# Where the side work of an attention unit stands on TensorE: two blocks, and three operands in the scores' rotation

## The chip, the core and the metric

The kernel runs on one core of a Trainium2 chip. The metric is device time in microseconds (us). Three runs of the kernel before gave 3573.38 us as their median (3570.64 to 3573.6). The engines are called PE (TensorE's matmuls), PEld (its weight loads), DVE (VectorE), ACT (ScalarE), POOL (GpSimd) and SP (SyncE, which issues DMAs here). They run side by side and wait for each other through semaphores.

## The reference

Two layers on x of shape (8, 2048, 256), with one matrix adj of 2048 x 2048. Layer 0 is a graph convolution with two linear maps and batch norms, and a layer norm of x plus its result. Layer 1 is masked attention with four heads, again with a residual and a layer norm:

```python
def _L1_gnn_ref(h, W, adj):
    ...
    qkv = h @ W
    qkv = qkv.reshape(Bn, Nn, 3, H, HEAD_DIM).transpose(2, 0, 3, 1, 4)
    q, k, v = (qkv[0], qkv[1], qkv[2])
    mask = jnp.where(adj == 0, -jnp.inf, 0.0)
    scores = jnp.einsum('bhid,bhjd->bhij', q, k) / np.sqrt(HEAD_DIM) + mask
    attn = jax.nn.softmax(scores, axis=-1)
    out = jnp.einsum('bhij,bhjd->bhid', attn, v)
    return out.transpose(0, 2, 1, 3).reshape(Bn, Nn, OUT_DIM)

# --- layer 0 (adj_resnorm) ---
x = _layernorm(x + _L0_gnn_ref(x, adj, ...), axis=-1)
# --- layer 1 (adj_resnorm) ---
x = _layernorm(x + _L1_gnn_ref(x, L1_gnn_W, adj), axis=-1)
```

All values are float32. The change touches layer 1 alone, and in it the end of layer 0's norm (its second linear map's result, called y, is normalised, added to x and layer-normalised inside the attention loop).

## The kernel before

The attention is cut into 64 *units*: 8 batches x 2 pairs of heads (hp) x 4 chunks (c) of 512 query rows. A unit has 16 *steps*, one for each 128 rows of keys, so there are 1024 steps g in all. In a step PE multiplies K and Q into a tile of scores (`scores`, L910: four matmuls in four 64 x 64 quarters of the array, eight records each step), DVE adds the mask (`mask_scores`, L922), ACT takes the exponential (L928), and three steps later (LEAD = 3) PE weighs V with it (`weigh`, L940, four quarters again). POOL adds up the probabilities for the softmax's sums (L950 to L961), with DMAs that add one tile into another.

PSUM, where PE writes, is full: the scores' tiles are `st` from the pool ps_s with two buffers of two banks each; the weighed sum is `out_ps` from ps_o with one buffer of two banks; everything else is `pm` from ps_m with two buffers of one bank each. A tile of a pool takes the place of the one before the last of its name, and waits until that one's readers have ended. Waits are kept by tile.

Beside that each unit has *side work*, in calls listed by `at_step(u, j, f, ...)`: the call is made in unit u at step int(j); calls of one step are sorted by j. If j is whole the call stands between the scores and their mask, otherwise behind the exponential. All engines but SP keep the order in which the program is written.

The side work on PE, all with the full height of the array, is:

- `finish_sums` (L977): the sums of the unit before, four matmuls with a 128 x 32 block of ones; ACT copies the result to sm (L985).
- `finish_turn_sums` (L991): two transposes of sm; DVE copies the sums and takes their reciprocal (L993, L998).
- `finish_turn` (L1004) and `finish` (L1012): four transposes of the unit's result ot, and eight small multiply-adds on DVE in two halves.
- `project` (L845 for Q and K, L859 for V): Q, K and V of a later chunk from the turned input x1t. ACT empties Q (L850) and V (L866), DVE empties K (L854).
- `norm` (L779): y of the next batch is transposed in two halves of four transposes into a pm tile, and DVE adds x (L787) and takes the layer norm's statistics (L728, L730). `turn` (L808) transposes the normalised x; ACT copies it to x1t (L814).

In a steady unit these stood in up to four places: Q at step 0 (with the second half of y), sums, K and y's first half at step 6, the turning of sums, V and the turning of ot at step 10, and the turning of x at step 13. Where a unit ends, `finish_out` copies and adds the two halves of out_ps to ot on ACT and DVE (L965, L966) before the next unit's first weighing may overwrite them. The loop that sets the order is:

```python
if j == NT - 1:
    weigh(g)
    finish_out(u)
tasks = side.get((u, j), ())
for i, f, args in tasks:
    if i == j:
        f(*args)
if ahead:
    mask_scores(g + LEAD, st)
    exps(g + LEAD)
for i, f, args in tasks:
    if i > j:
        f(*args)
if j < NT - 1:
    weigh(g)
```

Of the kernel before, what the change touches and what calls it, by code (L numbers as in the profile page):

```python
# [8 lines left out]
F32 = mybir.dt.float32  # L9
# [17 lines left out]
def tile_gcn_then_masked_attention(  # L27
# [15 lines left out]
    nc = tc.nc  # L43
    ENG = mybir.EngineType
    PSUM = bass.MemoryType.PSUM
    P = 128
    B, N, D = x.shape
# [7 lines left out]
    CH = 512  # L55
    NCH = N // CH
    TPC = CH // P
    NALL = B * NCH
    HP = D // P
# [138 lines left out]
    with tc.tile_pool(name="bt7", bufs=1, side="right") as bp7, tc.tile_pool(  # L198
        name="stage", bufs=2, side="right"
    ) as sp, tc.tile_pool(name="stage1", bufs=1, side="right") as sp1, tc.tile_pool(  # L200
        name="pst", bufs=4, space=PSUM
# [17 lines left out]
        for n, t in enumerate(order):  # L219
# [9 lines left out]
            here = slice(q * P, (q + 1) * P)  # L229
# [52 lines left out]
    with tc.tile_pool(  # L282
        name="psa", bufs=4, space=PSUM
# [147 lines left out]
        for v, (k, b, d) in enumerate(units):  # L431
            first, last = v == 0, v == len(units) - 1
            turn = not last and units[v + 1][0] != k
            w = v + 1
# [114 lines left out]
        for name, size in (  # L549
            ("h1", [P, NH, CH]), ("dbc", [P, 2, CH]), ("w1f", [P, 4, H // 2])  # L550
        ):
            t = lp.tile(size, F32, name=name).rearrange("p a b -> p (a b)")
# [156 lines left out]
    IT = BR // P  # L709
    NU = B * HP * NCH  # L710
# [5 lines left out]
    class LayerNorm:  # L716
# [9 lines left out]
        def stats(self, tiles):  # L726
            for i in tiles:
                nc.vector.bn_stats(self.st[:, i, :], self.t[:, i, :])  # L728
            for i in tiles:
                nc.vector.bn_aggr(self.mv[:, i, :], self.st[:, i, :])  # L730
# [14 lines left out]
    class Layer1Input:  # L745
# [23 lines left out]
        def norm(self, b, c, half):  # L769
            pm = self.psum.tile([P, IT, D], F32, name="pm")  # L770
            self.turn_y(b, c, half, pm)
            self.add_y(b, c, half, pm, self.x1[b, c])

        def turn_y(self, b, c, half, pm):
            y = self.yt[b, c]
            for i in range(IT):
                r0 = (IT * half + i) * P
                for o in range(NO):
                    nc.tensor.transpose(  # L779
                        pm[:, i, o * P : (o + 1) * P], y[:, o, r0 : r0 + P], ident  # L780
                    )
# [31 lines left out]
            r0 = c * CH + half * BR  # L813
            nc.scalar.copy(self.x1t[b][:, :, r0 : r0 + BR], pm)  # L814

        def emit_stats(self, b, c, half):
            if half == 0:
                self.ln[b, c] = LayerNorm(self.pool, self.x1[b, c])
            self.ln[b, c].stats(range(IT * half, IT * (half + 1)))
# [8 lines left out]
            if half:  # L828
                nc.sync.dma_start(rows(b, c, out), self.x1.pop((b, c)))

        def project(self, b, hp, c, which, k_on_act=False):

            if (b, hp) not in self.qkv:
                self.qkv[b, hp] = (
                    self.pool.tile([P, N], F32, name="qt"),
                    self.pool.tile([P, N], F32, name="kt"),
                    self.pool.tile([P, NT, P], F32, name="v"),
                )
            xt = self.x1t[b]
            cols = slice(c * CH, (c + 1) * CH)  # L840
            wcols = slice(which * D + hp * P, which * D + (hp + 1) * P)
            pm = self.psum.tile([P, CH], F32, name="pm")
            if which < 2:
                for d in range(ND):
                    nc.tensor.matmul(  # L845
                        pm, wq[:, d, wcols], xt[:, d, cols], start=(d == 0), stop=(d == ND - 1)
                    )
                dst = self.qkv[b, hp][which][:, cols]
                if which == 0:
                    nc.scalar.activation(dst, pm, AF.Copy, scale=HD**-0.5)  # L850
                elif k_on_act:
                    nc.scalar.copy(dst, pm)
                else:
                    nc.vector.tensor_copy(dst, pm)  # L854
            else:
                for j in range(TPC):
                    t = c * TPC + j
                    for d in range(ND):
                        nc.tensor.matmul(  # L859
                            pm[:, j * P : (j + 1) * P],  # L860
                            xt[:, d, t * P : (t + 1) * P],
                            wq[:, d, wcols],
                            start=(d == 0),
                            stop=(d == ND - 1),
                        )
                nc.scalar.copy(  # L866
                    self.qkv[b, hp][2][:, c * TPC : (c + 1) * TPC, :].rearrange(
                        "p t d -> p (t d)"
                    ),
                    pm,  # L870
                )
# [5 lines left out]
    def attention():  # L877


        with tc.tile_pool(  # L880
            name="attn_in", bufs=2, side="left", reuse_waits="tile"
        ) as ip, ExitStack() as late, tc.tile_pool(
            name="ps_s", bufs=2, space=PSUM, reuse_waits="tile"
        ) as ps_s, tc.tile_pool(
            name="ps_o", bufs=1, space=PSUM, reuse_waits="tile"
        ) as ps_o, tc.tile_pool(
            name="ps_m", bufs=2, space=PSUM, reuse_waits="tile"
        ) as ps_m:
            inp = Layer1Input(ip, ps_m, NCH + 4)
# [148 lines left out]
            def at_step(u, j, f, *args):  # L1038
                tasks = side.setdefault((u, int(j)), [])
                tasks.append((j, f, args))  # L1040
                tasks.sort(key=lambda task: task[0])

            per_b = HP * NCH
            for u in range(NU):
                b, hp, c = units[u]
                at_step(u + 1, 6, finish_sums, u)
                at_step(u + 1, 10, finish_turn_sums, u)
                at_step(u + 1, 10.2, finish_turn, u)
                at_step(u + 1, 10.3, finish, u, 0)
                at_step(u + 1, 11.1, finish, u, 1)  # L1050
                if u == NU - 2:
                    for half in range(2):
                        at_step(u + 1, 11.3 + half, inp.emit_stats, b, c, half)
                        at_step(u + 1, 14 + half, inp.emit, b, c, half)
                    at_step(u + 1, 12.5, inp.root, b, c)
                elif u == NU - 1:
                    for half in range(2):
                        at_step(u + 1, 10.4 + half, inp.emit_stats, b, c, half)
                        at_step(u + 1, 10.5 + half, inp.root_half, b, c, half)
                        at_step(u + 1, 12 + half, inp.emit_half, b, c, half)  # L1060
                    at_step(u + 1, 14, count_sums)
                elif hp == HP - 1:
                    for half in range(2):
                        at_step(u + 1, 12.5 + 1.5 * half, inp.emit_stats, b, c, half)
                        at_step(u + 2, 4 + half, inp.emit, b, c, half)
                    at_step(u + 1, 15.5, inp.root, b, c)

            PROJECT = (0.2, 6.1, 10.1)  # L1070

            def project_at(u, b, hp, c):
                for w in range(3):
                    at_step(u, PROJECT[w], inp.project, b, hp, c, w)

            for b in range(B):
                u0 = b * per_b
                if b:
                    project_at(u0, b, 0, NCH - 1)
                for c in range(NCH):  # L1080
                    project_at(u0 + 1 + c, b, 1, c)
                    if b + 1 == B:
                        continue
                    u = u0 + 3 + c
                    at_step(u, 1, inp.load_y, b + 1, c)
                    at_step(u, 1, inp.load_x, b + 1, c)
                    for o in range(NO):
                        at_step(u, 3.5 + 1.2 * o, inp.bn, b + 1, c, o)
                    at_step(u, 6.2, inp.norm, b + 1, c, 0)
                    at_step(u + 1, 0.1, inp.norm, b + 1, c, 1)  # L1090
                    at_step(u + 1, 3, inp.root, b + 1, c)
                    for half in range(2):
                        at_step(u + 1, 7 + half, inp.apply, b + 1, c, half)
                        at_step(u + 1, 13 + 0.2 * half, inp.turn, b + 1, c, half)
                    if c < NCH - 1:
                        project_at(u + 2, b + 1, 0, c)

# [8 lines left out]
            ):  # L1106
                at_step(0, j, inp.project, 0, 0, c, w)
            for c in (2, 3):
                at_step(c - 1, 3.1, inp.project, 0, 0, c, 0)

            with tc.manual_schedule(engines=IN_ORDER):
                for c in range(NCH):
# [37 lines left out]
                for g in range(NU * NT):  # L1150
                    u, j = divmod(g, NT)
                    ahead = g + LEAD < NU * NT
                    if ahead:
                        st = scores(g + LEAD)
# [22 lines left out]
    def attention_with_maxima():  # L1177

        with tc.tile_pool(name="full", bufs=2) as ap_, tc.tile_pool(
            name="full_s", bufs=2, space=PSUM  # L1180
        ) as ps_s, tc.tile_pool(name="full_o", bufs=2, space=PSUM) as ps_o, tc.tile_pool(
            name="full_m", bufs=2, space=PSUM
# [5 lines left out]
            inp = Layer1Input(ap_, ps_m, NCH)  # L1188
            for b in range(B):
# [12 lines left out]
                for hp in range(HP):  # L1202
# [4 lines left out]
                    for t in range(NT):  # L1207
                        for h in range(2):
# [23 lines left out]
                            for j in range(NT):  # L1232
                                pm = ps_m.tile([P, P], F32, name="pm")
# [10 lines left out]
                            )  # L1244
                for c in range(NCH):
                    for half in range(2):
                        inp.emit_stats(b, c, half)
                    inp.root(b, c)
                    for half in range(2):
                        inp.emit(b, c, half)  # L1250

    attention()


    n_bad = nc.values_load(bad[0:1, 0:1])
    with tc.If(n_bad > 0):
        attention_with_maxima()
# [43 lines left out]
```

## Time and profile before

| What | us |
|---|---|
| Median of the runs | 3573.38 |
| The profiled execution, its own time | 3573.89 |
| Its span, from the first to the last instruction | 3571.8 |
| Busy: PE / DVE / ACT / POOL | 3524.8 / 2112.7 / 1575.7 / 2335.5 |
| L922, the masks on DVE, 1024 of 1.215 | 1239.1 |
| L928, the exponentials on ACT, 1024 of 1.056 | 1081.2 |
| L940 and L910, weighings and scores on PE | 1075.0 and 1063.6 |
| L845, Q and K; L859, V | 253.0; 125.1 |

The profile is one execution, recorded by instruction. The attention's first scores stand at 1251 us and its last weighings at 3542 us, so it holds some 2290 us of the span. Scores, weighings and the side work share PE. A float32 matmul is two records; a transpose is one. The four quarter matmuls of a step overlap, so that eight records of 0.59 us fill about 0.86 us. In timelines, a group's length runs to the modelled end of its last record and overlaps the next group; the distance from start to start is the time a group really takes of PE. Idle time in square brackets is that of the engine before the group, with what ended it.

### The profile page before, as it was taken

The numbers are of one execution on the slowest core, as the hardware profiler recorded it, in microseconds if no ns is written. First come the engines' busy times: TensorE is split into PE (matmuls) and PEld (weight loads), VectorE is DVE, ScalarE is ACT, GpSimd is POOL, SyncE is SP. The second block draws the span as 40 slices with busy tenths as digits, with TensorE's granted clock in tenths as the row PEclk, the third lists the DMA queues.
The fourth block names the chain that finished last, engine by engine and source line by source line (L and its number), as shares of the span: only waits on it lengthen the run. The fifth ranks groups of instructions, "written<-read, shape, count | busy, mean of one in ns | idle before, by whom it ended". The sixth has DMA issues, their size and how long they took to land. (4 is left out here: it accounts for less than half of the span.)

```text
span 3571.8 us, 55309 instructions
## 1 busy us (share of the span) xinstructions
PE 3524.8 (99%) x22447; PEld 1461.9 (41%) x22447; DVE 2112.7 (59%) x3125; ACT 1575.7 (44%) x1952; POOL 2335.5 (65%) x1590
## 2 busy tenths in 40 slices
PE   8999999999999899999999999999999999999997
PEld 5444444444444433433343433343443334343332
DVE  6224342432356656766766776676676676676666
ACT  5000000000045455665665565565566565566555
POOL 4544364435357556777777787777677777777777
PEclk9999999999999899999999999999999999999999
DMA  9122242231256445666575566566556556655555
GB/s 342 53 77 81 90 159 71 71 100 41 77 228 241 152 83 108 129 126 123 111 149 117 115 130 134 110 137 129 114 124 142 110 122 137 120 114 122 113 113 114
DMA packets 197577, 440.16 MB, mean 123 GB/s; under 512 B 14128, under 2 KB 121152, under 8 KB 186944
## 3 DMA queue, kind: packets, MB, share of 16 engines
q0 software_dynamic: 64656, 239.37, 35.3%
q1 hardware_dynamic: 132048, 196.11, 16.0%
q8 instruction: 178, 2.92, 0.3%
q10 hardware_dynamic: 608, 1.06, 0.1%
q14 instruction: 87, 0.71, 0.1%
HBM read 126.62 MB, written 75.51 MB: 57 GB/s over the span
## 5 line engine op out<-in xcount | busy, mean ns | idle before, releaser
L922 DVE SCALAR_TENSOR_TENSOR prob<-mask,st 128x1024 f32<-128x1024 uint8 x1024 | 1239.1, 1215 | 434.5 <-PE st L910 360.6
L928 ACT ACTIVATE prob<-prob 128x1024 f32<-128x1024 f32 x1024 | 1081.2, 1056 | 913.5 <-DVE prob L922 836.3
L940 PE MATMUL out_ps<-prob,v 64*64 64x512 f32 x8192 | 1075.0, 595 | 3.6 <-DVE ot L966 2.6
L910 PE MATMUL st<-qt,kt 64*64 64x512 f32 x8192 | 1063.6, 589 | 0.1
L961 POOL TENSOR_TENSOR acc<-acc,prob 128x1024 f32<-128x1024 f32 x319 | 830.0, 2602 | 5.7 <-DMA prob<-prob 0.7
L341 PE MATMUL pa<-t,x 128*128 128x512 f32 x1792 | 774.5, 594 | 2.7 <-ACT x L317 2.7
L950 POOL DMA_DIRECT2D prob<-prob x447 | 403.8, 929 | 565.3 <-PE out_ps L940 458.0
L910 PEld LDWEIGHTS st<-qt,kt 64*64 64x64 f32 x8192 | 312.6, 133 | 566.7 <-issue 526.9
L341 PEld LDWEIGHTS pa<-t,x 128*128 128x128 f32 x1792 | 342.1, 191 | 431.9 <-issue 427.7
L940 PEld LDWEIGHTS out_ps<-prob,v 64*64 64x64 f32 x8192 | 290.9, 133 | 542.1 <-issue 469.4
L952 POOL TENSOR_TENSOR acc<-acc,prob 128x1024 f32<-128x1024 f32 x126 | 298.1, 2365 | 7.5
L845 PE MATMUL pm<-x1t,wq 128*128 128x512 f32 x512 | 253.0, 617 | 0.7 <-ACT x1t L814 0.7
L470 POOL TENSOR_TENSOR ag<-ag,dbc 128x512 f32<-128x512 f32 x16 | 20.2, 1263 | 314.5 <-DVE ag L469 287.9
L450 ACT COPY ag<-pa 128x512 f32<-128x512 f32 x16 | 9.4, 588 | 448.2 <-PE pa L341 435.1
L399 ACT COPY h<-ph 128x512 f32<-128x512 f32 x28 | 16.4, 585 | 416.7 <-PE ph L390 416.7
L959 POOL TENSOR_TENSOR acc<-prob 128x1024 f32<-128x1024 f32 x64 | 171.1, 2674 | 3.0 <-DMA prob<-prob 3.0
L740 ACT ACTIVATE x<-x,ln_nm,ln_rs 128x256 f32<-128x256 f32 x256 | 137.6, 586 | 8.7 <-POOL ln_nm L736 8.7
L845 PEld LDWEIGHTS pm<-x1t,wq 128*128 128x128 f32 x512 | 87.9, 191 | 119.5 <-issue 112.8
L1012 DVE SCALAR_TENSOR_TENSOR x<-pm,ri,x 128x64 f32<-128x64 f32 x512 | 109.5, 277 | 44.1 <-PE pm L1004 44.1
L859 PE MATMUL pm<-wq,x1t 128*128 128x128 f32 x1024 | 125.1, 276 | 0.0
L859 PEld LDWEIGHTS pm<-wq,x1t 128*128 128x128 f32 x1024 | 119.4, 192 | 2.5 <-ACT x1t L814 1.7
L966 DVE TENSOR_TENSOR ot<-out_ps,ot 128x512 f32<-128x512 f32 x64 | 44.3, 692 | 124.4 <-ACT ot L965 124.4
(156 smaller groups left out, 2855.8 us busy)
## 6 DMA issues: line engine op xcount, KB each, us to landing
prob<-prob POOLq DMA_DIRECT2D x447, 512.0 KB, 4.9
x<-in_x_dram SPq DMA_DIRECT2D x92, 512.0 KB, 6.6
h_d<-h SPq DMA_DIRECT2D x28, 1024.0 KB, 4.2
t<-h_d SPq DMA_DIRECT2D x28, 1024.0 KB, 7.5
a<-in_adj_dram SPq DMA_DIRECT2D x16, 1024.0 KB, 5.0
y_d<-ag SPq DMA_DIRECT2D x32, 512.0 KB, 2.6
out_dram<-x SPq DMA_DIRECT2D x31, 512.0 KB, 6.8
yt<-y_d SPq DMA_DIRECT2D x28, 512.0 KB, 3.2
```

What stands on the lines that cost most here:

```text
L341: nc.tensor.matmul(pa, s.t[:, m, :], t[:, m, :], start=(m == 0), stop=(m == HT - 1))
L740: nc.scalar.activation(self.t[:, i, :], self.t[:, i, :], AF.Identity, bias=self.nm[:, i : i + 1], scale=self.rs[:, i : i + 1],)
L845: nc.tensor.matmul(pm, wq[:, d, wcols], xt[:, d, cols], start=(d == 0), stop=(d == ND - 1))
L859: nc.tensor.matmul(pm[:, j * P : (j + 1) * P], xt[:, d, t * P : (t + 1) * P], wq[:, d, wcols], start=(d == 0), stop=(d == ND - 1),)
L910: nc.tensor.matmul(st[r * HD : (r + 1) * HD, h, :], kt[hs, j * P + r * HD : j * P + (r + 1) * HD], qt[hs, cols], start=True, stop=True,)
L922: nc.vector.scalar_tensor_tensor(p, mask[:, j, cols][:, None, :].to_broadcast([P, 2, CH]), MASKED, st, op0=ALU.mult, op1=ALU.add,)
L928: nc.scalar.activation(probs[g], probs[g], AF.Exp)
L940: nc.tensor.matmul(outs[u][hs, r, :], inp.qkv[b, hp][2][rs, j, hs], probs[g][rs, h, :], start=(j == 0), stop=(j == NT - 1),)
L950: nc.gpsimd.dma_start(probs[g - 1], probs[g], accum_op=ALU.add)
L952: nc.gpsimd.tensor_add(accs[u], accs[u], probs[g])
L959: nc.gpsimd.tensor_add(accs[v], probs[g - 7], probs[g - 5])
L961: nc.gpsimd.tensor_add(accs[v], accs[v], probs[g - 5])
```

## The change

It moves side work and changes three of its PSUM tiles. What moves:

- The sums' turning, V's projection and ot's turning go from step 10 to step 6, behind the sums and K, so that step 6 holds all of them in one run: L977, K, L991, V, L1004. In the lists of units 61 to 64 (the constant BARE = 61), where no projection is left, turning and finishing stay at steps 10 and 11.
- Q's projection goes from step 0 to 15.2, that is behind the unit's last weighing; for the last chunk of a batch's second pair of heads it goes to 6.6 instead.
- y's two halves are transposed together, behind the last weighing (15.1), by the new `turn_and_add`, first both transposes, then both additions. The turning of x goes from step 13 to 15, the layer norm's statistics to steps 0.1 and 1.1 of the next unit, and the scaling from steps 7 and 8 to 9 and 11.
- K and V share one tile of the scores' name `st` (K in its first half, V in its second), and both halves of y take one such tile, in place of pm tiles.
- The statistics of a finished chunk move to 9.1 and 10.6, its root to 12.5, and its output's scaling and DMA from step 4 to steps 1 and 2 of the unit behind.

`emit_stats` is only renamed to `stats`.

```diff
+        def turn_and_add(self, b, c, pm):
+
+            for half in range(2):
+                self.turn_y(b, c, half, pm[:, IT * half : IT * (half + 1)])
+            for half in range(2):
+                here = slice(IT * half, IT * (half + 1))
+                t = self.x1[b, c][:, here]
+                nc.vector.tensor_add(t, pm[:, here], t)
...
-        def project(self, b, hp, c, which, k_on_act=False):
+        def project(self, b, hp, c, which, k_on_act=False, pm=None):
...
-            pm = self.psum.tile([P, CH], F32, name="pm")
+            if pm is None:
+                pm = self.psum.tile([P, CH], F32, name="pm")
...
+            spare = {}
+
+            def key_projection(u, b, hp, c):
+                spare[u] = ps_s.tile([P, 2, CH], F32, name="st")
+                inp.project(b, hp, c, 1, pm=spare[u][:, 0, :])
+
+            def value_projection(u, b, hp, c):
+                inp.project(b, hp, c, 2, pm=spare.pop(u)[:, 1, :])
+
+            def norm(b, c):
+                inp.turn_and_add(b, c, ps_s.tile([P, TPC, D], F32, name="st"))
+
             per_b = HP * NCH
+
+            BARE = NU - NCH + 1
             for u in range(NU):
                 b, hp, c = units[u]
                 at_step(u + 1, 6, finish_sums, u)
-                at_step(u + 1, 10, finish_turn_sums, u)
-                at_step(u + 1, 10.2, finish_turn, u)
-                at_step(u + 1, 10.3, finish, u, 0)
-                at_step(u + 1, 11.1, finish, u, 1)
+                if u + 1 < BARE:
+                    at_step(u + 1, 6.2, finish_turn_sums, u)
+                    at_step(u + 1, 6.4, finish_turn, u)
+                    at_step(u + 1, 6.5, finish, u, 0)
+                    at_step(u + 1, 7.1, finish, u, 1)
+                else:
+                    at_step(u + 1, 10, finish_turn_sums, u)
+                    at_step(u + 1, 10.2, finish_turn, u)
+                    at_step(u + 1, 10.3, finish, u, 0)
+                    at_step(u + 1, 11.1, finish, u, 1)
...
+                elif hp == HP - 1 and u + 1 < BARE:
+                    for half in range(2):
+                        at_step(u + 1, 9.1 + 1.5 * half, inp.stats, b, c, half)
+                        at_step(u + 2, 1.05 + half, inp.emit, b, c, half)
+                    at_step(u + 1, 12.5, inp.root, b, c)
...
-            PROJECT = (0.2, 6.1, 10.1)
...
             def project_at(u, b, hp, c):
-                for w in range(3):
-                    at_step(u, PROJECT[w], inp.project, b, hp, c, w)
+                last = hp == HP - 1 and c == NCH - 1
+                at_step(u, 6.6 if last else 15.2, inp.project, b, hp, c, 0)
+                at_step(u, 6.1, key_projection, u, b, hp, c)
+                at_step(u, 6.3, value_projection, u, b, hp, c)
...
-                    at_step(u, 6.2, inp.norm, b + 1, c, 0)
-                    at_step(u + 1, 0.1, inp.norm, b + 1, c, 1)
+                    at_step(u, 15.1, norm, b + 1, c)
                     at_step(u + 1, 3, inp.root, b + 1, c)
                     for half in range(2):
-                        at_step(u + 1, 7 + half, inp.apply, b + 1, c, half)
-                        at_step(u + 1, 13 + 0.2 * half, inp.turn, b + 1, c, half)
+                        at_step(u + 1, 0.1 + half, inp.stats, b + 1, c, half)
+                        at_step(u + 1, 9 + 2 * half, inp.apply, b + 1, c, half)
+                        at_step(u + 1, 15, inp.turn, b + 1, c, half)
...
-                at_step(c - 1, 3.1, inp.project, 0, 0, c, 0)
+                at_step(c - 2, (15.2, 6.6)[c - 2], inp.project, 0, 0, c, 0)
```

More of the change, by code (lines that the diff above doesn't have):

```diff
@@ L814, in turn, with stats @@
             nc.scalar.copy(self.x1t[b][:, :, r0 : r0 + BR], pm)
-        def emit_stats(self, b, c, half):
+        def stats(self, b, c, half):
             if half == 0:
@@ L1046, in attention @@
                 at_step(u + 1, 6, finish_sums, u)
-                at_step(u + 1, 10, finish_turn_sums, u)
-                at_step(u + 1, 10.2, finish_turn, u)
-                at_step(u + 1, 10.3, finish, u, 0)
-                at_step(u + 1, 11.1, finish, u, 1)
+                if u + 1 < BARE:
[8 more added lines that the diff above has]
+                    at_step(u + 1, 11.1, finish, u, 1)
                 if u == NU - 2:
                     for half in range(2):
-                        at_step(u + 1, 11.3 + half, inp.emit_stats, b, c, half)
+                        at_step(u + 1, 11.3 + half, inp.stats, b, c, half)
                         at_step(u + 1, 14 + half, inp.emit, b, c, half)
@@ L1057, in attention @@
                     for half in range(2):
-                        at_step(u + 1, 10.4 + half, inp.emit_stats, b, c, half)
+                        at_step(u + 1, 10.4 + half, inp.stats, b, c, half)
                         at_step(u + 1, 10.5 + half, inp.root_half, b, c, half)
@@ L1061, in attention @@
                     at_step(u + 1, 14, count_sums)
+                elif hp == HP - 1 and u + 1 < BARE:
[3 more added lines that the diff above has]
+                    at_step(u + 1, 12.5, inp.root, b, c)
                 elif hp == HP - 1:
                     for half in range(2):
-                        at_step(u + 1, 12.5 + 1.5 * half, inp.emit_stats, b, c, half)
+                        at_step(u + 1, 12.5 + 1.5 * half, inp.stats, b, c, half)
                         at_step(u + 2, 4 + half, inp.emit, b, c, half)
                     at_step(u + 1, 15.5, inp.root, b, c)
-            PROJECT = (0.2, 6.1, 10.1)
             def project_at(u, b, hp, c):
-                for w in range(3):
-                    at_step(u, PROJECT[w], inp.project, b, hp, c, w)
+                last = hp == HP - 1 and c == NCH - 1
+                at_step(u, 6.6 if last else 15.2, inp.project, b, hp, c, 0)
+                at_step(u, 6.1, key_projection, u, b, hp, c)
+                at_step(u, 6.3, value_projection, u, b, hp, c)
             for b in range(B):
@@ L1246, in attention_with_maxima @@
                     for half in range(2):
-                        inp.emit_stats(b, c, half)
+                        inp.stats(b, c, half)
                     inp.root(b, c)
```

## The prediction

> **What bounds the kernel now.** I read the totals first, then the stages, then the order of work on PE inside one attention unit, then the waits.
>
> ```profile
> PE 3524.8 (99%) x22447; PEld 1461.9 (41%) x22447; DVE 2112.7 (59%) x3125; ACT 1575.7 (44%) x1952; POOL 2335.5 (65%) x1590
> L940 PE MATMUL out_ps<-prob,v 64*64 64x512 f32 x8192 | 1075.0, 595 | 3.6 <-DVE ot L966 2.6
> ```
>
> PE is busy 99% of the span, and the weighing line sat idle 3.6 us in 8192 records. The table of stages says the same of the attention alone:
>
> ```profile
> 2000.00:2500.00 500.00, 499.26 (x4195) 198.24 (x4197) 345.98 (x523) 302.62 (x368) 375.57 (x269) 1.00 0.62 127
> ```
>
> Columns after the window: its length, then busy PE, PEld, DVE, ACT, POOL. PE has 0.7 us free of 500, at full clock. So the time is PE's own: its work, what it loses between kinds of work, and any wait that is new. The busy number hides the losses, since matmuls overlap; they show in the starts. PE's timeline (start, length, line, shape, records):
>
> ```profile
> 2006.48 1.04 PE L940 MATMUL out_ps<-prob,v 64*64 64x512 f32 x8
> 2007.34 1.04 PE L910 MATMUL st<-qt,kt 64*64 64x512 f32 x8
> 2008.30 0.44 PE L991 MATMUL pm<-ident,sm 128*128 128x128 f32 x2
> 2008.58 1.95 PE L859 MATMUL pm<-wq,x1t 128*128 128x128 f32 x16
> 2010.36 0.60 PE L1004 MATMUL pm<-ident,ot 128*128 128x128 f32 x4
> 2010.89 1.09 PE L940 MATMUL out_ps<-prob,v 64*64 64x512 f32 x8
> 2011.80 1.04 PE L910 MATMUL st<-qt,kt 64*64 64x512 f32 x8
> ...
> 2021.57 1.04 PE L910 MATMUL st<-qt,kt 64*64 64x512 f32 x8
> 2022.54 0.66 PE L779 MATMUL pm<-ident,yt 128*128 128x128 f32 x4
> 2023.03 1.88 PE L845 MATMUL pm<-x1t,wq 128*128 128x512 f32 x4
> 2024.84 1.09 PE L940 MATMUL out_ps<-prob,v 64*64 64x512 f32 x8
> ...
> 2034.34 1.04 PE L910 MATMUL st<-qt,kt 64*64 64x512 f32 x8
> 2035.31 0.64 PE L977 MATMUL pm<-acc,ones 128*32 128x256 f32 x8
> 2035.87 1.99 PE L845 MATMUL pm<-x1t,wq 128*128 128x512 f32 x4
> 2037.69 0.60 PE L779 MATMUL pm<-ident,yt 128*128 128x128 f32 x4
> 2038.22 1.09 PE L940 MATMUL out_ps<-prob,v 64*64 64x512 f32 x8
> ```
>
> Scores and weighings follow each other every 0.86 us. Full-array side work begins 0.97 instead of 0.86 after the scores before it (0.11 lost), and the first 64x64 group behind it lasts 0.91 (0.05 lost). K's projection takes 1.82 before a transpose, and 1.92 before a weighing (3368.94 to 3370.86). DVE's timeline shows who empties K, and what follows a unit's last weighing:
>
> ```profile
> 2022.43 0.69 DVE L966 TENSOR_TENSOR ot<-out_ps,ot 128x512 f32<-128x512 f32 x1 [1.97 <-ACT ot L965]
> 2023.04 2.34 DVE L922 SCALAR_TENSOR_TENSOR prob<-mask,st 128x1024 f32<-128x1024 uint8 x2
> ...
> 2037.90 0.69 DVE L854 COPY kt<-pm 128x512 f32<-128x512 f32 x1 [1.16 <-PE pm L845]
> ```
>
> The copy of kt starts 2.03 us after K's first matmul (2035.87), after 1.16 us of idle DVE: it is bound by PE alone. Over all units 1 to 60 that distance is 2.02 and the copy 0.69.
>
> **What the Trainium skill says.** "TensorEngine Tiling (Array Packing)", Tiling Modes, Key Properties: changing the tiling mode drains TensorE. The trace agrees: about 0.16 us per excursion at its two edges, and about 0.1 more where it ends in a projection. "Perfetto Trace Analysis", Optimizing Tensor Performance, Matmuls: independent matmul groups should rotate through PSUM banks, so that the emptying of one overlaps the next. Before does this with two pm tiles, and none of the 60 V projections there carries a wait. "PSUM — Partial Sum Buffer", the section on bank collisions: access to different banks runs clean (no run here tests it). K's and V's halves are one bank each, so the hardware asks for no order between them; what the program waits for is another matter (below). The same page, Engine vs sequencer instructions: matmuls start and complete in program order. So one waiting V holds up the transposes, the weighing and the scores behind it; no run yet shows that here.
>
> **The change part by part.** I counted side work between 64x64 groups for units 1 to 60, in the instruction order of both programs, and took the medians of the excursions in the trace (time from the scores before to the weighing behind, less 0.86).
>
> *Removed:* step 10 (L991, L859, L1004) 60 x 2.701 = 162.1. Step 6: 32 x 2.593 (L977, L845) + 28 x 3.029 (with half of y, L779) = 167.8, and 7 of the 28 wait 0.588 for ACT's sm: 4.1. Q alone 34 x 2.023 = 68.8; half of y with Q 28 x 2.416 = 67.6; turning x (L808) 28 x 1.132 = 31.7. First group behind each: 210 x 0.051 = 10.7. Sum 512.8 us.
>
> *Added, if nothing waits:* the block at step 6 from the starts above: 0.10 in, 0.56 sums, 1.82 K, 0.28 turning sums, 1.78 V, 0.53 turning ot = 5.08; 51 times, and 9 times with Q behind it 6.85: 320.7. Behind the last weighing: Q alone 26 x 2.02; y and Q 7 x 2.95; x, y and Q 14 x 4.02; x and y 7 x 2.21; x and Q 7 x 2.95; together 165.7. Behind each 121 x 0.051 = 6.2. Sum 492.6. So the regrouping itself is worth **-20.2 us**. The joints of the block are sums of measured joints, not measured: below, the block cannot be shorter than its streaming, some 4.74 (20 us more gain); above, it costs its two old excursions, 5.29 (12.6 less). I take 5.08, as each joint stands in the lines above.
>
> *Added wait:* K goes to one half and V to the other half of one st tile. In the changed program's order the first V matmul carries a wait for DVE's counter at the copy of kt out of that tile, in all 60 units; in before V has its own pm tile and no wait. K starts at 0; turning the sums ends at 1.82 + 0.28 = 2.10; the copy ends at 2.02 + 0.69 = 2.71, and a matmul starts 0.05 behind what released it (L779 starts 0.05 behind sm, 7 times). V starts at some 2.77 instead of 2.10: 0.67 lost. Nothing else stands there for PE: behind V in its queue are ot's transposes, the weighing and the next scores. A restart after a wait also loses the overlapped weight load: 0.06 on those transposes, 0.27 on a weighing behind ot (3461.45 to 3462.58 against 0.86); I take 0.10, a matmul's entry. 60 x 0.77 = **+46.2 us** (bounds 60 x 0.67 = 40 and 60 x 0.87 = 52).
>
> *The rotation elsewhere.* With a third tile, the scores behind a block meet the mask written one scores earlier. At step 6 the mask starts 1.1 behind the scores and lasts 1.2, the block lasts over 5: hidden. The tile of K and V is reused two scores later, over 2.5 us behind V; ACT's copy needs 0.8. Behind the last weighing (time 0, 2021.57 above) ot's add and the mask end at 2.7. Blocks of 2.95 and 4.02 hide that; x and y (2.21) wait 0.5, 7 times: +3.5. Q behind x alone needs a pm tile that ACT empties at 1.45 instead of 1.18: 7 x 0.3 = +2.1. The two adds on y end at 4.0, the next use of their tile is at 4.5 or later. The Q blocks leave the st order alone.
>
> *Moved at no cost:* masks back to back take 1.13 and with two tiles' statistics 2.0, against 1.72 a step; I followed DVE behind both blocks, it catches up before its st tile is due (0.5 us to spare at the nearest). SP's order and DMAs stay; yt is free earlier. POOL's accumulation needs 3.43 us per pair against 3.44 for two steps, now without the pauses at steps 10 and 13; in before 1.96 us at the least lay between the end of an addition and the mask that reuses its prob buffer, and POOL itself idled 3.2 us at the pause at step 10, so that its ends move up too. Gone, these covers would cost tenths of a us a unit.
>
> **Sum.** -20.2 + 46.2 + 3.5 + 2.1 = +31.6 us. The profiled execution took 3573.89 us (span 3571.8, 2.1 around it), the median is 3573.38: 3605.5 for the one, **3605 us** for the other.
>
> **The rivals.** (a) *The V wait is covered*: turning the sums or a late sm fills the gap. Then 3573.4 - 20.2 + 5.6 = 3559, faster. For it: PE's regrouping is certain work saved. Against: 0.28 us of transposes stand against 0.95 of latency and copy, and the copy starts 2.02 behind K in every unit. It decides if the wait is below (20.2 - 5.6)/60 = 0.24 us a unit. 4%. (b) *Joining saves nothing inside a block*, only the 89 returns (4.5) and sm's waits (4.1): +46.2 + 5.6 - 8.6 = +43, 3617. For it: the losses may belong to each kind of matmul and not to the edges; against: S and K alone are 0.68 and 2.02, together 2.59. 12%. (c) *The rotation waits more than I followed*, through DVE or POOL, some 0.35 us at each of 88 blocks that take a tile: +31 more, 3636. Against: the margins above. 8%. (d) The block reaches its streaming time: 20 us more gain, 3585, still slower, or with (a) in part no change: 3%.
>
> **How the numbers follow.** The forecast has 73%; its own range is 3592 to 3616 (wait 40 to 52, regrouping -14 to -26, rotation 0 to 8). To leave no more than 2 in 10 out I take in (b) and half of (d): 3588 to 3619. About 0.2%, 7 us, is what a measurement of this kernel tells from no change. Slower 0.93 (forecast, b, c, most of d), same 0.03, faster 0.04.
>
> **What would show it.** Right: V's matmuls wait for DVE's kt some 0.6 to 0.8 us, 60 times, 40 us or more in the waits of PE and PEld; excursions 135 instead of 225; the step 6 block near 5.85; ot blocks unchanged in the last three units. Wrong: V behind the sums' transposes within 0.1 us; plain pitches over 0.95 many times (rotation); a step 6 block, less its wait, of 5.3 (rival b).

## The result, and the profile after

| Kernel | Median, us | Ratio to before, 95% interval |
|---|---|---|
| before, same chip runs | 3572.22 (4 runs) | |
| changed | 3599.09 (4 runs) | 1.0073 [1.006, 1.0086] |

The change costs 26.9 us; 31.6 were forecast, and 3599 us lies inside the forecast's range of 3592 to 3616. The profiled execution took 3597.41 us with a span of 3595.3 (before: 3573.89 and 3571.8).

The page's totals of the changed kernel, and its groups of V's projection (line, engine, operation, operands, count | busy, mean ns | idle before, releaser):

```profile
PE 3510.2 (98%) x22447; PEld 1478.9 (41%) x22447; DVE 2105.7 (59%) x3125; ACT 1585.3 (44%) x1952; POOL 2341.5 (65%) x1590
L869 PE MATMUL st<-wq,x1t 128*128 128x128 f32 x960 | 123.1, 281 | 33.9 <-DVE kt L864 33.9
L869 PEld LDWEIGHTS st<-wq,x1t 128*128 128x128 f32 x960 | 111.7, 191 | 48.2 <-DVE kt L864 48.2
```

PE runs the same 22447 records with 15 us less of busy time in a span that is 23.5 us longer. V's projection (960 records = 60 units x 16) is idle before it for DVE's copy of kt, which it never was before. The table of stages puts the new idle time into the attention; the window is the one shown for the kernel before, where PE was busy 499.26 us of 500:

```profile
2000.00:2500.00 500.00, 490.11 (x4148) 201.02 (x4144) 340.05 (x520) 302.51 (x367) 368.75 (x266) 1.00 0.62 127
```

PE's list of waits names the groups before which PE stood idle, with the total, the count and the longest, in us. The changed kernel's lines are numbered some ten higher: L855 is Q's and K's projection, L864 DVE's copy of kt, L869 V, L920 the scores, L932 the mask.

```profile
PE st L869 <- DVE kt L864: 33.9, 60, 0.6
...
PE st L920 <- DVE prob L932: 5.3, 7, 0.8
...
PE pm L855 <- ACT x1t L823: 2.3, 8, 0.7
```

The first line is the wait of step 6, in all 60 units that have it. The second is the mask behind ot's addition, where x and y stand behind the last weighing without Q (7 blocks). The third holds Q behind x, in 7 blocks, and one more. The block of step 6 in PE's timeline (start, length, what) and DVE's copy beside it:

```profile
2001.34 1.04 PE L920 MATMUL st<-qt,kt 64*64 64x512 f32 x8
2002.31 0.64 PE L987 MATMUL pm<-acc,ones 128*32 128x256 f32 x8
2002.88 1.98 PE L855 MATMUL st<-x1t,wq 128*128 128x512 f32 x4
2004.70 0.38 PE L1001 MATMUL pm<-ident,sm 128*128 128x128 f32 x2
2005.64 2.05 PE L869 MATMUL st<-wq,x1t 128*128 128x128 f32 x16 [0.56 <-DVE kt L864]
2007.53 0.60 PE L1014 MATMUL pm<-ident,ot 128*128 128x128 f32 x4
```

```profile
2004.90 0.69 DVE L864 COPY kt<-st 128x512 f32<-128x512 f32 x1 [1.16 <-PE st L855]
```

K starts at 2002.88, its copy 2.02 later; V starts 0.05 behind the copy's end, at 2005.64, 2.76 behind K. The bracket shows 0.56 of idle PE only, because a group's length runs past the moment at which the next could start; the starts give the full price. In all 60 blocks V starts 0.05 behind the end of that copy. Then V takes 1.89 up to ot's transposes, where it took 1.78 in before.

### The profile page after: what moved, and what is told of

It is laid out like the page before. It is cut to its first block, busy times and chain, and to the rows that moved or that the text cites. A ratio compares the mean times of both kernels' runs of the same rounds, so it can differ in the third digit from the quotient of the medians.

```text
span 3595.3 us, 55462 instructions
## 1 busy us (share of the span) xinstructions
PE 3510.2 (98%) x22447; PEld 1478.9 (41%) x22447; DVE 2105.7 (59%) x3125; ACT 1585.3 (44%) x1952; POOL 2341.5 (65%) x1590
## 5 line engine op out<-in xcount | busy, mean ns | idle before, releaser
L932 DVE SCALAR_TENSOR_TENSOR prob<-mask,st 128x1024 f32<-128x1024 uint8 x1024 | 1242.0, 1218 | 423.2 <-PE st L920 421.5
L920 PE MATMUL st<-qt,kt 64*64 64x512 f32 x8192 | 1067.1, 591 | 5.4 <-DVE prob L932 5.3
L920 PEld LDWEIGHTS st<-qt,kt 64*64 64x64 f32 x8192 | 308.9, 133 | 578.4 <-issue 473.7
L950 PEld LDWEIGHTS out_ps<-prob,v 64*64 64x64 f32 x8192 | 307.8, 133 | 547.5 <-issue 491.4
L869 PE MATMUL st<-wq,x1t 128*128 128x128 f32 x960 | 123.1, 281 | 33.9 <-DVE kt L864 33.9
L855 PE MATMUL pm<-x1t,wq 128*128 128x512 f32 x272 | 131.6, 607 | 2.3 <-ACT x1t L823 2.3
L869 PEld LDWEIGHTS st<-wq,x1t 128*128 128x128 f32 x960 | 111.7, 191 | 48.2 <-DVE kt L864 48.2
L855 PE MATMUL st<-x1t,wq 128*128 128x512 f32 x240 | 119.0, 618 | 0.0
```

The lines of the kernel that those rows point to most:

```text
L855: nc.tensor.matmul(pm, wq[:, d, wcols], xt[:, d, cols], start=(d == 0), stop=(d == ND - 1))
L869: nc.tensor.matmul(pm[:, j * P : (j + 1) * P], xt[:, d, t * P : (t + 1) * P], wq[:, d, wcols], start=(d == 0), stop=(d == ND - 1),)
L920: nc.tensor.matmul(st[r * HD : (r + 1) * HD, h, :], kt[hs, j * P + r * HD : j * P + (r + 1) * HD], qt[hs, cols], start=True, stop=True,)
L932: nc.vector.scalar_tensor_tensor(p, mask[:, j, cols][:, None, :].to_broadcast([P, 2, CH]), MASKED, st, op0=ALU.mult, op1=ALU.add,)
L950: nc.tensor.matmul(outs[u][hs, r, :], inp.qkv[b, hp][2][rs, j, hs], probs[g][rs, h, :], start=(j == 0), stop=(j == NT - 1),)
```

## The experiments

Each was timed against the kernel before in the same chip job. A *block* (an excursion, in the forecast's words) is one run of side work between two 64x64 groups, scores or a weighing. Its time is the distance from the start of the group before it to the start of the group behind it, less the 0.86 us that a 64x64 group takes by itself.

**K in a tile of its own** (`k_own_pm`). V keeps its place in an st tile; K goes to a pm tile as in before:

```diff
             def key_projection(u, b, hp, c):
-                spare[u] = ps_s.tile([P, 2, CH], F32, name="st")
-                inp.project(b, hp, c, 1, pm=spare[u][:, 0, :])
+                inp.project(b, hp, c, 1)

             def value_projection(u, b, hp, c):
-                inp.project(b, hp, c, 2, pm=spare.pop(u)[:, 1, :])
+                st = ps_s.tile([P, 2, CH], F32, name="st")
+                inp.project(b, hp, c, 2, pm=st[:, 1, :])
```

> K goes to a pm tile of its own, V stays in the second half of an st tile; order, engines and copies as in the changed kernel. Theory (V waits because K and V share one tile): V's matmuls start 2.10 us behind K's first instead of 2.76 and take 1.78 instead of 1.89 up to the transposes of ot, so the block of step 6 falls from 5.87 to about 5.09; 60 x 0.77 = 46 us less than the changed kernel, 3553 us, some 19 us under the kernel before. Rival 1 (the stall belongs to V's place in an st tile, whose last reader is a mask): nothing changes, 3599. Rival 2 (joining kinds of work saves nothing by itself): the wait goes but the block stays near 5.3, 3565.

Measured: 3551.43 us, ratio 0.9937 [0.9924, 0.9951], 47.7 us under the changed kernel (49.1 when each is taken against the kernel before in its own job). PE's timeline of one block:

```profile
2026.83 0.64 PE L987 MATMUL pm<-acc,ones 128*32 128x256 f32 x8
2027.40 1.98 PE L855 MATMUL pm<-x1t,wq 128*128 128x512 f32 x4
2029.22 0.38 PE L1001 MATMUL pm<-ident,sm 128*128 128x128 f32 x2
2029.44 1.95 PE L869 MATMUL st<-wq,x1t 128*128 128x128 f32 x16
2031.22 0.60 PE L1014 MATMUL pm<-ident,ot 128*128 128x128 f32 x4
```

V starts 2.04 behind K, without a wait, and takes 1.78. DVE's copy of kt runs beside it (2029.42 to 2030.11). Over the 51 blocks without Q the median block is 5.035 us, against 5.865 in the changed kernel, and the 9 blocks with Q lose the same: 60 x 0.83 = 49.8 us. Rival 1 falls, for V stands where it stood. Rival 2 falls for this block, for 5.035 is not 5.3.

**V in a tile of its own** (`v_own_pm`): K stays in the st tile, V goes to pm.

```diff
             def value_projection(u, b, hp, c):
-                inp.project(b, hp, c, 2, pm=spare.pop(u)[:, 1, :])
+                spare.pop(u)
+                inp.project(b, hp, c, 2)
```

> V goes to a pm tile, K stays in the first half of the st tile. Theory: the same 46 us come back, less some 2 us because Q at step 6.6 of 9 units then waits for ACT's copy of V out of its pm tile: 3554 to 3555. Rival 1 (V's place in st): also about 3554, so this run alone does not tell it from the theory; with the run in which only K moves it does. Rival 3 (V waits for DVE's copy wherever it writes, since the order on the engines asks for it): 3599.

Measured: 3554.14 us, ratio 0.9947 [0.9932, 0.9962]. The wait for kt is gone here too, so it belongs to neither operand's place but to the two sharing a tile; rival 3 falls. The 9 blocks with Q take 7.257 instead of 6.754 us, as Q now needs the pm tile that ACT must empty of V: 4.5 us by the trace, where 2 were expected.

**ot's transposes ahead of V** (`ot_between`): K and V share the tile.

```diff
-                    at_step(u + 1, 6.4, finish_turn, u)
+                    at_step(u + 1, 6.25, finish_turn, u)
```

> K and V share the st tile as in the changed kernel, but the four transposes of ot stand before V and not behind it. Theory (V waits for a fixed moment, the end of kt's copy, 2.76 us behind K's first matmul): the transposes fill 0.53 us of it, the wait falls from 0.66 to about 0.14, and V pays 0.10 more where a weighing follows it: block 5.42 instead of 5.87, 60 x 0.44 = 27 us less, 3572. Rival 4 (the cost is a fixed price of any wait on PE, not the gap): within 5 us of 3599.

Measured: 3574.28 us, ratio 1.0002 [0.9993, 1.001].

```profile
1997.14 1.98 PE L855 MATMUL st<-x1t,wq 128*128 128x512 f32 x4
1998.96 0.38 PE L1001 MATMUL pm<-ident,sm 128*128 128x128 f32 x2
1999.18 0.60 PE L1014 MATMUL pm<-ident,ot 128*128 128x128 f32 x4
1999.91 2.05 PE L869 MATMUL st<-wq,x1t 128*128 128x128 f32 x16
```

```profile
1999.16 0.69 DVE L864 COPY kt<-st 128x512 f32<-128x512 f32 x1 [1.16 <-PE st L855]
```

V starts 2.77 behind K, as in the changed kernel (2.76), although about half a microsecond more of work stands ahead of it, and again 0.05 behind the end of kt's copy, in all 60 blocks. So what holds V is a moment, the end of kt's copy. The median block is 5.428 us (5.42 expected): the loss falls from 0.83 to 0.39 a block, and rival 4, one price for any wait, falls. A small part does stay whatever the gap: in the 9 blocks where Q follows V, V runs 1.89 behind this shorter wait too, against 1.79 without one. PE's list of waits has no line for kt here, because the length of ot's group covers the gap; V's weight loads (PEld) show it, idle 22.0 us for kt in 60 blocks. That cover alone brings the kernel back to the time of before.

**Step 6's block alone** (`block6_alone`), in the kernel before, with K in pm and V in half an st tile. The turning and finishing move for the same units as in the change.

```diff
-                at_step(u + 1, 10, finish_turn_sums, u)
-                at_step(u + 1, 10.2, finish_turn, u)
...
+                    at_step(u + 1, 6.2, finish_turn_sums, u)
+                    at_step(u + 1, 6.4, finish_turn, u)
...
-            PROJECT = (0.2, 6.1, 10.1)
...
+                at_step(u, 0.2, inp.project, b, hp, c, 0)
+                at_step(u, 6.1, inp.project, b, hp, c, 1)
+                at_step(u, 6.3, value_projection, b, hp, c)
...
-                    at_step(u, 6.2, inp.norm, b + 1, c, 0)
+                    at_step(u, 6.7, inp.norm, b + 1, c, 0)
```

> The kernel before with step 6's block alone: turning of sums, V and turning of ot behind K at step 6, K in pm, V in half an st tile, y's first half behind ot at 6.7; Q, y's second half and the turning of x at their old places. Theory (losses belong to the edges of excursions and to the joints): 60 x (2.593 + 2.701 + 0.051 - 5.09) = 15 us saved, 4 us of waits for sm gone, 2 us more for y's half: 3555. Rival 2 (joining saves nothing in a block): 60 x 0.05 = 3 us and the 4 us of waits: 3565.

Measured: 3555.46 us, ratio 0.9947 [0.9933, 0.9961]. Joining saves what the edges and joints say: 5.034 us for what cost 2.593 + 2.701 and one more return of 0.05, which is 0.31 a block or 18.7 us, where 15 were expected. In 7 of the 28 blocks with y PE still waits for sm, as in before (6.07 us instead of 5.47), so the 4 us of these waits were not gained as expected.

**The second block alone** (`block15_alone`), in the kernel before: Q, y and x behind the last weighing, y's halves in an st tile, statistics and scalings of the next batch as in the change; the last chunk's Q stays at step 0, and a finished chunk's statistics stay at their old steps.

```diff
+                last = hp == HP - 1 and c == NCH - 1
+                for w, j in enumerate((0.2 if last else 15.2, 6.1, 10.1)):
+                    at_step(u, j, inp.project, b, hp, c, w)
...
-                    at_step(u, 6.2, inp.norm, b + 1, c, 0)
-                    at_step(u + 1, 0.1, inp.norm, b + 1, c, 1)
+                    at_step(u, 15.1, norm, b + 1, c)
...
-                        at_step(u + 1, 13 + 0.2 * half, inp.turn, b + 1, c, half)
...
+                        at_step(u + 1, 15, inp.turn, b + 1, c, half)
```

> The kernel before with the second block alone: Q, both halves of y (in an st tile) and the turning of x behind the last weighing, with the statistics and scalings moved as in the changed kernel; sums, K, V and ot at steps 6 and 10 as before, each in a pm tile; Q of a batch's last chunk stays at step 0. Theory, from the excursions of both traces: behind the last weighing 14 x 3.73 + 7 x 2.85 + 7 x 2.83 + 7 x 3.36 = 115.4 us, against 28 x 2.416 + 28 x 1.132 + 28 x 0.436 + 4.1 = 115.7 in before, and 28 returns of 0.05 us fewer: 1.7 us less, 3570.5, no change that can be measured. Rival 5 (every excursion removed is worth the same, 28 of 90): some 6 to 7 us less, 3565.

Measured: 3575.07 us, ratio 1.0006 [0.9998, 1.0015]: no change to be measured. The trace holds 202 blocks against 223 in before, so 21 excursions are gone and not the 28 of the expectation. Rival 5 falls as a forecast of the time, but not because an excursion is worth nothing. Set beside the same blocks without their waits (2.007 and 2.851 us, in the last two runs below), the 21 excursions give 6.5 us, 0.31 each as at step 6, and 4.1 us of waits for sm go too. New waits take it all back: the mask holds the scores behind x and y, 7 x 0.82 = 5.8 us, and Q waits behind x, 7 x 0.86 = 6.0 us. The second of these was dearer than expected: a block of x with Q takes 3.71 us, against 3.36 in the changed kernel. PE's timeline, and ACT's:

```profile
2128.47 1.04 PE L949 MATMUL out_ps<-prob,v 64*64 64x512 f32 x8
2129.44 1.09 PE L817 MATMUL pm<-ident,x 128*128 128x128 f32 x8
2131.13 1.98 PE L854 MATMUL pm<-x1t,wq 128*128 128x512 f32 x4 [0.60 <-ACT x1t L823]
```

```profile
2129.06 1.06 ACT L937 ACTIVATE prob<-prob 128x1024 f32<-128x1024 f32 x1 [0.93 <-DVE prob L931]
2130.02 0.57 ACT L974 COPY ot<-out_ps 128x512 f32<-128x512 f32 x1
2130.49 1.08 ACT L823 COPY x1t<-pm 128x512 f32<-128x512 f32 x2
```

Q waits for ACT's copy of x out of the pm tile; ACT is late, since its exponential waited for a mask. DVE's timeline has a finished chunk's statistics between its last masks, at their old steps 12.5 and 14 (2124.95 and 2126.96, a microsecond each, 4.5 and 2.5 us before the block). In the changed kernel they start 9.8 and 7.8 us before such a block, and ACT is done with its exponential before the last weighing ends. So these statistics are the likely cause, but no run moved them alone.

**The mask before ot's addition** (`mask_first`), on the kernel with K in its own tile:

```diff
+                    early = j == NT - 1 and u + 1 < BARE - 1
                     if j == NT - 1:
                         weigh(g)
+                        if early:
+                            mask_scores(g + LEAD, st)
                         finish_out(u)
...
-                        mask_scores(g + LEAD, st)
+                        if not early:
+                            mask_scores(g + LEAD, st)
```

> The kernel with K in its own pm tile, and at a unit's last step (units up to 58) the mask three steps ahead is written before DVE adds ot's halves, not behind. Theory (the 7 blocks of x and y wait for the mask, since it stands behind ot's add, which waits for ACT's copy): the mask then ends at about 1.5 us behind the last weighing instead of 2.7, those blocks fall from 2.83 to about 2.2: 7 x 0.6 = 4 us less than 3551.4, 3547; all other blocks stay. Rival 6 (ot's later add, now ending near 2.2, delays the next unit's first weighing, which may not overwrite out_ps): Q blocks of 2.02 put that weighing at 2.9, so nothing, but if ACT or DVE run later than that, up to 0.5 us in 40 units, 3570.

Measured: 3542.72 us, ratio 0.992 [0.9906, 0.9934]: 8.7 us under the kernel with K in its own tile, 6.7 when each is taken against the kernel before in its own job, where 4 were expected. The changed kernel's block of x and y, and the same one here:

```profile
2026.25 1.10 PE L817 MATMUL pm<-ident,x 128*128 128x128 f32 x8
2027.18 1.04 PE L788 MATMUL st<-ident,yt 128*128 128x128 f32 x8
2028.97 1.09 PE L920 MATMUL st<-qt,kt 64*64 64x512 f32 x8 [0.75 <-DVE prob L932]
```

```profile
2008.00 1.09 PE L817 MATMUL pm<-ident,x 128*128 128x128 f32 x8
2008.93 1.04 PE L788 MATMUL st<-ident,yt 128*128 128x128 f32 x8
2009.89 1.09 PE L920 MATMUL st<-qt,kt 64*64 64x512 f32 x8
```

The scores follow 0.96 instead of 1.79 behind y's transposes: 2.007 against 2.830 us a block (2.2 expected), 7 x 0.82 = 5.8 us. Rival 6 falls: no weighing waits more than before.

**Q beside x in an st tile** (`best`), on top of that, for the 7 blocks with x and Q:

```diff
+            def query_projection(b, hp, c):
+                st = ps_s.tile([P, 2, CH], F32, name="st")
+                inp.project(b, hp, c, 0, pm=st[:, 0, :])
...
+                if hp == 0 and c == NCH - 2:
+                    at_step(u, 15.2, query_projection, b, hp, c)
+                else:
+                    at_step(u, 6.6 if last else 15.2, inp.project, b, hp, c, 0)
```

> The same, and Q of the 7 blocks with x and Q goes to half an st tile instead of a pm tile, so that it no longer waits for ACT's copy of x out of that pm tile. Theory: these blocks fall from 3.36 to about 2.86, as y and Q: 7 x 0.5 = 3.5 us less than the run with the mask first, 3543.5. Rival 7 (the scores behind the block then wait for the mask in the other st tile, or two scores later for Q's copy): the gain is lost, 3547.

Measured: 3539.59 us, ratio 0.9911 [0.9897, 0.9925]. The 7 blocks fall from 3.355 to 2.851, 3.5 us in all as expected, and rival 7 falls. The table of stages for the same window as above:

```profile
2000.00:2500.00 500.00, 500.00 (x4276) 203.84 (x4272) 352.37 (x529) 308.57 (x372) 382.73 (x274) 1.00 0.63 129
```

PE is never free in it. This version is faster than both kernels: 32.1 us below its runs of the kernel before.

## Why the prediction was right

- **The place of the loss.** The forecast put it on V's wait for kt's copy, through the shared tile: 60 waits, V starting some 2.77 behind K. The trace has 60 waits and 2.76, and the first two experiments take the loss away by separating the operands, whichever of the two moves. Rival (a), a covered wait, is excluded in the changed kernel; `ot_between` shows what covering would have taken.
- **Its size.** 60 x 0.77 = 46.2 forecast, 60 x 0.83 = 49.8 measured. The start of V without a wait was put at 2.10 behind K; it is 2.04. Two transposes take 0.22 between projections, and the 0.28 of the sum was read where they followed a 64x64 group. The restart cost 0.10 (1.89 against 1.79, medians of 60), as was taken; but that was a choice between two readings, 0.06 and 0.27, and came out by luck.
- **The regrouping at step 6.** 5.08 forecast, 5.035 measured without the wait, and 6.85 against 6.754 with Q: 3.2 us better over 60 blocks. Rival (b), a block of 5.29, is excluded, and so is (d): the block is far from 4.74. That bound stands in the forecast without its working.
- **The blocks behind the last weighing.** x, y and Q: 3.73 instead of 4.02, 14 times. y and Q: 2.85 instead of 2.95. The working took 1.03 to 1.07 for eight transposes; between a 64x64 group and other full-array work they take 0.93, and 0.87 behind other transposes. The waits were larger than put: x and y took 2.83 instead of 2.71, x and Q 3.36 instead of 3.25. Together 3.2 us better. Q alone stands there 25 times, not 26: 2.0 us less. That was a slip of the count, for the forecast takes out 62 projections of Q and puts in 63.
- **The sum.** 31.6 + 3.6 - 3.2 - 3.2 - 2.0 = 26.8 us. The excursions of the two traces, with the first group behind each, differ by 26.8 us, the medians by 26.9.
- **The rotation and POOL.** Rival (c) did not come: outside the 7 blocks of x and y no scores waited for a mask, and plain distances between 64x64 groups stay between 0.86 and 0.91 but for the three unit ends that waited in before too.
- **What the whole held.** Step 6's block is worth 18 us alone; the second block alone is worth nothing that can be measured, although it removes 21 excursions. With both and the wait gone the gain is 22 us: by the traces, the nine projections of Q that then join step 6's block save some 3.6 us more, and x with Q is 2.5 us cheaper than in `block15_alone`.

## What to carry to other kernels

Where waits are kept by tile, as here, two operands that share one tile share its waits: the second write waits for the first one's reader, though the halves are different banks. Before putting an operand into a free half, ask what work stands on the writing engine between the first operand's end and its copy's end, and whether that covers latency and copy (here 0.22 us of 0.94).

A saturated engine gains from joining its side work where a full-array stretch is entered and left less often: here about 0.31 us for each stretch saved, in both blocks. A few new waits can eat that, as in `block15_alone`, so a count of stretches is not the gain; follow each joint for what its first instruction waits for, and read the result from starts, group by group. And where the work between two waits shrinks or moves, look at the order on the engine that releases them: one mask put ahead of one addition was worth 6 us here.

## What the runs showed of the hardware that was not expected

- The price of a transpose depends on its neighbours. Eight 128x128 float32 transposes take 0.87 us between other full-array work (14 blocks of x, y and Q), 0.93 behind a 64x64 group (2026.25 to 2027.18), and 1.03 between two 64x64 groups (2016.20 to 2017.23 in before). So the 0.06 and the 0.10 go with the step from and to 64x64 groups, not with the transposes. Projections show the same 0.10 before a 64x64 group (1.82 against 1.92), and behind one: Q before scores takes 1.81 behind transposes and 1.91 behind a weighing. That the change of tiling is the cause fits all of these, but no run changes the tiling alone.
- A projection that waited runs slower afterwards: V lost 0.10 us of its own running behind the wait in every block, beside the 0.73 by which it started late, and Q behind x takes 1.91 with its wait and 1.81 without it (`best`). The scores that waited for a mask do not show this (0.88 to the next group, against 0.91).
- Idle time before a group can hide a wait. In the changed kernel it shows 0.56 of the 0.73 us by which V starts late; in `ot_between` it shows nothing, where V starts 0.73 behind ot's transposes, which take 0.44 before another projection: 0.29 us lost, 60 times.
